# Second batch of a gated attention and expert kernel: another order of its query tiles, one more pair by seven products, and two tiles scored in one step

## The chip, the core and the metric

The kernel runs on one core of one Trainium2 chip. The core has a matrix engine (TensorE, PE in the profile), a vector engine (VectorE, DVE), a scalar engine (ScalarE, ACT), a general engine (GpSimd, POOL) and a synchronisation engine (SyncE, SP), which here issues nearly all the loads, stores and transposes by DMA. Each engine executes its own list of instructions in order and waits on semaphores for the others. The metric is device time in microseconds; the median of three runs before the change is 1007.83 us (1007.52 to 1008.42).

## What is computed

The input x has two batches of 2,048 tokens with 512 features. It is normalised twice over; causal attention with one head of width 512 and an output projection is taken of it, a mixture of eight experts (two per token) gives a gate, and the output is x plus attention times the gate:

```python
scores = jnp.einsum('bsk,btk->bst', q, k) * scale
scores = jnp.where(causal[None], scores, -jnp.inf)
attn = jax.nn.softmax(scores, axis=-1)
out = attn @ v
...
xn = _layernorm(x, axis=-1)
s = _L0_attn_ref(xn, ...)
g = _silu(_L0_ffn_ref(xn, ...))
x = x + s * g
```

Everything is computed in 32-bit floats. The change concerns the attention of the second batch only: `scores`, `attn` and `attn @ v`.

## The kernel before

**Stages.** The tokens are cut into 32 tiles of 128, sixteen to a batch, and into eight blocks of 512, four to a batch. Projections come first (queries, keys and values go to DRAM), then the routing, then the experts, and from about 550 us on the attention. The list of every engine is written out by hand: the order of the Python statements is the order of the instructions on each engine.

**The steps of the attention.** A loop (L1760) goes over steps `s` = 0 to 37. The list `seq` (L1014, L1015) says which query tile a step handles: steps 0 to 15 take the first batch from tile 15 down to tile 0, steps 16 to 31 the second batch in an order of its own. Steps go in pairs of neighbouring tiles, and pair numbers (`s // 2`) run from 0 to 15. Tile t of a batch needs t + 1 tiles of keys, so it has t + 1 units of score work and t + 1 units of value work.

**One plain step.** `chunk_scores` (L1302) multiplies the step's queries with a block of 512 keys, or what of it lies below the diagonal, into a PSUM bank of pool `ps_a` (five banks). VectorE masks the last 128 columns (L1312) and takes the maximum (L1295); `end_scores` (L1393) joins the maxima. `exponentials` (L1478) has ScalarE write the probabilities (L1485), POOL split them into 16-bit halves (L1495) and SP transpose them by DMA (L1501). In the step after, VectorE joins the transposed halves (`join_p`, L1515). Two steps after its scores, `values` (L1522) multiplies the transposed probabilities with the values into a bank of `ps_b` (three banks). The three smallest tiles are transposed by TensorE instead (`turn_p`, L1508).

**The end of a tile.** Three steps after its scores a tile is scaled (`attended`, L1693: ScalarE, then VectorE); in the step after that POOL multiplies and adds (`emit`, L1704) and SP stores. Every second step POOL gathers the experts' rows of a pair (`gather_y`, L1671), and later ScalarE and VectorE make the gate of them (`gate`, L1683), with a silu, for which ScalarE changes its table of functions.

**Seven products.** Pairs listed in `SCORED` (L1271) have the scores of their first 1,024 keys made by `fast_scores` (L1342). It takes the 2 x 2 blocks of a product (two query tiles by two key blocks, the 512 features in two halves) and makes seven half-size products in place of eight, from sums of the queries (`query_sums`, L1320, VectorE) and of two key blocks (`block_sums`, L1331). Pairs in `FAST` (L1272), which are those of `SCORED` and pair 4, have their values made by seven products too: `combine_v` (L1548) makes sums of a value block, `combine_p` (L1559) sums of the probabilities, and `values_first`, `values_next` and `values_end` (L1604 to L1622) the products and additions.

**Loads and sums in advance.** `parts_b` (L1740) lists the steps in which the second batch's key and value blocks are loaded, four parts a step; `later` (L1746) lists the steps in which their sums are made. Each entry names the steps of the four sums, the function and the block; K is the first block of the second batch.

Of the kernel before, what the change touches and what calls it, by code (L numbers as in the profile page):

```python
# [26 lines left out]
def gated_attention_moe(  # L27
# [32 lines left out]
    NT = B * S // P  # L60
    BT = 4
    TB = BT * P
    NB = NT // BT
    NBB = S // TB
# [947 lines left out]

    assert B == 2 and NBB == 4
    seq = [t for t in reversed(range(NBB * BT))]  # L1014
    seq += [NBB * BT + t for t in (8, 9, 0, 1, 6, 7, 2, 3, 4, 5, 10, 11, 12, 13, 14, 15)]  # L1015
    assert all(seq[s] // 2 == seq[s + 1] // 2 for s in range(0, NT, 2))
    fetch_k = fetch(aks, lambda: kp2, kt_d, "k2", "kT")
    fetch_v = fetch(avs, lambda: vp, v_d, "v2", "v")
# [249 lines left out]
    OUT = 4  # L1268


    SCORED = (0, 1, 2, 3, 13, 14, 15)  # L1271
    FAST = SCORED + (4,)  # L1272

    def place(s):
        b, t = divmod(seq[s], BT)
        return b, t, b - b % NBB
# [21 lines left out]
    def direct(s):  # L1298

        return range(2 if s // 2 in SCORED else 0, len(widths[s]))  # L1300

# [91 lines left out]
    def end_scores(s):  # L1393
        mx, nm, pieces = scored[s]
        nc.vector.tensor_reduce(nm, mx[:, : len(pieces)], AX.X, ALU.max, negate=True)  # L1395
# [82 lines left out]
    def exponentials(s):  # L1478

        _, nm, pieces = scored.pop(s)  # L1480
        rs = sm.tile([P, NBB], F32, name=f"rs_{s}", tag="rs")
        sums[s], halves[s] = rs[:, : len(pieces)], []
        for j, (src, at) in enumerate(pieces):
            end = at + src.shape[1]
            nc.scalar.activation(  # L1485
                turned[s][:, at:end], src, AF.Exp, bias=nm, accum_out=rs[:, j : j + 1]
            )
            if by_te(s):
                continue
            for k in range(at, end, TB):  # L1490
                w = min(end - k, TB)

                pool, tag, n = (op, "xo", 4) if s == 1 else (php, "pu", 3)
                pu = pool.tile([P, 2 * TB], U16, name=f"pu_{s}_{k}", tag=tag, bufs=n)
                nc.gpsimd.tensor_copy(  # L1495
                    pu[:, : 2 * w].rearrange("p (h d) -> p h d", h=2),
                    turned[s][:, k : k + w].bitcast(U16).rearrange("p (d h) -> p h d", h=2),
                )
                pool, tag, n = (op, "o", 4) if s == 1 else (php, "puT", 5)
                puT = pool.tile([P, 2 * BT, P], U16, name=f"puT_{s}_{k}", tag=tag, bufs=n)  # L1500
                nc.sync.dma_start_transpose(out=puT[:, : 2 * w // P, :], in_=pu[:, : 2 * w])  # L1501
                halves[s].append((puT, k, w))

    def by_te(s):

        return sum(widths[s]) <= 3 * P
# [186 lines left out]
    def attended(s):  # L1693
        n = seq[s]
        o = outs[s] if s // 2 in FAST else op.tile([P, D], F32, name=f"o_{s}", tag="o", bufs=4)
        nc.scalar.activation(  # L1696
# [42 lines left out]
    K = NBB  # L1739
# [6 lines left out]
    later = {}  # L1746
    for steps, f, b in (
        ((10, 10, 11, 11), combine_v, K + 2), ((12, 12, 13, 13), combine_v, K + 1),
        ((20, 21, 22, 23), block_sums, K), ((24, 25, 26, 27), combine_v, K),
    ):  # L1750
        for i, step in enumerate(steps):
            later.setdefault(step, []).append((f, b, (i + 1,)))
# [6 lines left out]

    for s in range(NT + OUT + 2):  # L1760
        fast = s // 2 - 1 in FAST
        pair = (s, s + 1) if s // 2 in SCORED else (s,)
        if s < NT and (s % 2 == 0 or len(pair) == 1):
            for k in pair:
                if s:
                    begin_scores(k)
                room(k)
        n = s // 2 + 1
        if s % 2 == 0 and NQ <= n < NT // 2:
            for c in range(2):  # L1770
                fetch_q(n, c)
        if s == 0:
            fetch_parts(s, NBB * ND)
            block_sums(0)
        late = []
        for k in range(NT):
            if k not in AHEAD:
                wait = 4 - k % 2 if k // 2 in FAST else 3
                if s == k + wait:
                    late.append((attended, k))  # L1780
                if s == k + wait + 1:
                    emit(k)
        if s == NT:

            values_first(s - 2)
            for k in AHEAD:
                make_ahead(k)
        if len(pair) == 1 or s % 2:
            for f, *args in late:
                f(*args)  # L1790
        for k in range(NT):
            if s == (NT - 1 if k in AHEAD else k + 2 - k % 2 if k // 2 in FAST else k + 1):
                fetch_inputs(k)
        if s == NT - 1:
            gather_y(NT - 2)
        if s % 2 and s > 3 and s // 2 + 1 in SCORED:
            query_sums(s + 1, nc.vector)
        joins = []
        for k in () if s == 1 else (0, 1) if s == 2 else (s - 1,):
            if 0 <= k < NT - 1 and not by_te(k):  # L1800
                joins += [(join_p, k)] * len(halves[k])
        chunks = []
        if s < NT and s != 1:
            chunks = [(k, j) for k in ((1,) if s == 0 else (s,)) for j in direct(k)]
        if s == 0:

            for k, j in chunks:
                chunk_scores(k, j)
            chunks = []
        if s < NT and s % 2 == 0 and len(pair) == 2:  # L1810
            pools = [(ps_a, "a")] * 5 + [(ps_b, "b"), (ps_a, "a")]
            if s < 3:
                pools = [(ps_b, "b")] * 3 + [(ps_a, "a")]
            if s == 2:
                joins = [(combine_v, b, (1,)) for b in range(NBB - 1)] + joins
            now = 5 if s == 2 else 1
            fast_scores(s, pools, late + joins[:now])
            joins = joins[now:]
            if s == 0:
                query_sums(2, nc.gpsimd)  # L1820
        for k, j in chunks:
            chunk_scores(k, j)
            if s != 3 and joins:
                f, *args = joins.pop(0)
                f(*args)
        if s != 3:
            for f, *args in joins:
                f(*args)
        if 0 <= s - 1 < NT and by_te(s - 1):

            if not fast:
                values(s - 2)
            turn_p(s - 1)
        if s < NT and s != 1:
            end_scores(s)
        if fast and s % 2 == 0 and 2 < s < NT:
            combine_p(s - 2)
        if 0 <= s - 1 < NT:
            divisor(s - 1)
        if s < NT:  # L1840
            if s != 1:
                exponentials(s)
            if s % 2 == 0 and len(pair) == 2:
                maximum(s + 1, turned[s + 1][:, : 2 * TB], 0)
            if s == 0:
                end_scores(1)
                exponentials(1)
            fetch_parts(s, 4)
            for f, *args in later.pop(s, []):
                f(*args)  # L1850
        if s == 2:
            pass
        elif s == 3:
            combine_p(0, (1, 3, 2))
            for b in range(NBB - 1):
                combine_v(b, (2,))
            values_first(0)
            combine_p(0, (4,))
            for b in range(NBB - 1):
                combine_v(b, (4,))  # L1860
            values_next(0)
            for f, *args in joins:
                f(*args)
            values_end(0, [lambda: query_sums(s + 1, nc.vector)])
        elif s == NT:
            emit_ahead(s - 2, seven[s - 2][1], LO)
            values_next(s - 2)
        elif fast and s % 2 == 0:
            values_first(s - 2)

            if s != NT - 2:
                values_next(s - 2)
        elif fast and s == NT - 1:
            values_next(s - 3)
            values_end(
                s - 3,
                [lambda: join_p(s)] * len(halves[s])
                + [lambda: combine_p(s - 1, (1, 3)), lambda: gate(s - 1)]
                + [lambda: combine_p(s - 1, (2, 4))],
            )  # L1880
        elif fast:
            values_end(s - 3)
        elif 0 <= s - 2 < NT and not (s - 1 < NT and by_te(s - 1)):
            values(s - 2)

        for k in range(0, NT - 2, 2):
            if s == (k + 2 if k + 2 in AHEAD else k + 3):
                gate(k)
        for k in range(0, NT - 2, 2):
            if s == k + 1:  # L1890
                gather_y(k)
        if s == 1:

            for b in (2, 0, 1):
                combine_v(b, (3,), nc.gpsimd)
# [45 lines left out]
```

## Time and profile before

The page shows one profiled execution. Its span is from the first to the last instruction; its own time is the device time of the same execution.

| what | value |
|---|---|
| median of three runs | 1007.83 us |
| profiled execution, its own time | 1007.83 us |
| its span | 1006.0 us |
| span outside the attention's last part | 0 to 568 us: TensorE busy 566.38 us |
| 568 to 777.3 us (the first batch's attention) | TensorE 208.65, VectorE 152.46, ScalarE 66.69, POOL 109.62 us of 209.3 |
| 777.3 to 865.6 us (the second batch's first ten steps) | TensorE 88.30, VectorE 53.45, ScalarE 43.02, POOL 66.69 us of 88.3 |
| 865.6 to 1002.2 us (its last six tiles) | TensorE 136.60, VectorE 103.32, ScalarE 45.28, POOL 66.48 us of 136.6 |

In the rows of the profile, L1307 stands for score work of a plain step, L1359 for the seven products of scores, L1535 for plain value work and L1583 for the seven products of values. A group such as "x8" of one score block has two rows for each matmul of 32-bit floats. An idle time in brackets names the engine and line that ended it.

### The profile page before, as it was taken

How to read it: one execution, taken by the hardware profiler on the slowest of the kernel's cores; microseconds unless marked ns; L12 is line 12 of the kernel's file. 1: busy time of each engine (PE TensorE's matmuls, PEld its weight loads, DVE VectorE, ACT ScalarE, POOL GpSimd, SP SyncE). 2: the span in 40 equal slices, each digit the busy share in tenths (PEclk: the TensorE clock that was granted, in tenths of full speed). 3: DMA queues.
4: the chain of work that ended last, by engine and by line, in shares of the span. 5: the costliest groups of instructions: out<-in, count | busy, mean ns of one | idle time of the engine just before them, and what ended most of it. 6: DMA issues, size and time to landing. Idle time of an engine off the chain costs nothing. (4 is left out here: it accounts for less than half of the span.)

```text
span 1006.0 us, 13431 instructions
## 1 busy us (share of the span) xinstructions
PE 999.9 (99%) x3924; PEld 665.3 (66%) x3924; DVE 716.9 (71%) x1396; ACT 403.2 (40%) x804; POOL 483.3 (48%) x475
## 2 busy tenths in 40 slices
PE   9999999999999999999999999999999999999998
PEld 5888888874567767766753448677675544447577
DVE  6996746897887777677744579668576556878667
ACT  3344445322444454444445112232335535442241
POOL 4474564004644454444332165254557776764272
PEclk9999999999999999999999999999999999999999
DMA  8689996978999999999999576274677768753361
GB/s 293 193 264 293 329 286 258 349 249 240 202 227 220 211 208 221 217 200 222 216 218 242 164 193 147 78 206 104 183 199 239 225 200 240 207 141 86 92 165 42
DMA packets 296647, 207.96 MB, mean 207 GB/s; under 512 B 230776, under 2 KB 243832, under 8 KB 296576
## 3 DMA queue, kind: packets, MB, share of 16 engines
q1 hardware_dynamic: 282432, 163.56, 63.2%
q0 software_dynamic: 10400, 34.63, 12.5%
q10 hardware_dynamic: 3744, 8.91, 2.4%
q8 instruction: 34, 0.56, 0.2%
q14 instruction: 37, 0.30, 0.1%
HBM read 92.35 MB, written 60.03 MB: 151 GB/s over the span
## 5 line engine op out<-in xcount | busy, mean ns | idle before, releaser
L1195 PE MATMUL py<-arena,ht 128*128 (+3 forms) x396 | 176.7, 593 | 0.0
L1307 PE MATMUL ps<-k,q 128*128 128x512 f32 (+3 forms) x416 | 143.0, 495 | 0.3 <-PEq L1455 0.3
L1495 POOL COPY pu<-pT 128x1024 uint16<-128x1024 uint16 (+2 forms) x74 | 82.5, 1146 | 118.1 <-ACT pT L1485 59.1
L1166 POOL COPY hu<-h 128x704 uint16<-128x704 uint16 x66 | 61.9, 956 | 155.8 <-issue 121.7
L1195 PEld LDWEIGHTS py<-arena,ht 128*128 128x128 f32 (+3 forms) x396 | 71.8, 185 | 80.7 <-issue 76.9
L1307 PEld LDWEIGHTS ps<-k,q 128*128 128x128 f32 x416 | 74.7, 190 | 67.1 <-issue 56.5
L970 POOL DMA_INDIRECT xs<-zu_d,toki x66 | 77.6, 1176 | 70.2 <-DVE toki L791 55.6
L1181 ACT ACTIVATE ht<-ht,b1sel 128x128 f32<-128x128 f32 (+3 forms) x216 | 67.9, 380 | 88.1 <-DVE ht L1175 88.1
L1145 DVE TENSOR_TENSOR h<-p,h 128x176 f32<-128x176 f32 x182 | 55.5, 337 | 60.7 <-PE p L1138 57.2
L1678 POOL DMA_INDIRECT yg<-y_d,posi x64 | 67.4, 1053 | 36.9 <-DVE yg L1689 21.9
L1535 PE MATMUL po<-v,pT 128*128 128x512 f32 x152 | 67.9, 592 | 0.0
L347 POOL COPY zu<-z 128x1024 uint16<-128x1024 uint16 x32 | 39.9, 1245 | 55.7 <-DVE z L332 55.7
L1517 DVE COPY pT<-puT 128x1024 uint16<-128x1024 uint16 (+2 forms) x74 | 54.1, 759 | 8.8 <-DMA puT<-pu 8.6
L1485 ACT ACTIVATE pT<-pT,nm 128x1024 f32<-128x1024 f32 x14 | 16.1, 1148 | 110.3 <-DVE nm L1395 72.0
L1203 ACT COPY y<-py 128x512 f32<-128x512 f32 x55 | 32.2, 585 | 62.3 <-PE py L1195 48.4
L1485 ACT ACTIVATE pT<-ps,nm 128x512 f32<-128x512 f32 (+3 forms) x52 | 30.1, 581 | 62.5 <-DVE nm L1395 38.8
L1365 DVE TENSOR_TENSOR pT<-p,pT 128x512 f32<-128x512 f32 x49 | 32.9, 687 | 25.8 <-PE p L1359 22.1
L1535 PEld LDWEIGHTS po<-v,pT 128*128 128x128 f32 x152 | 28.6, 190 | 31.9 <-issue 30.1
L1707 POOL TENSOR_TENSOR o<-o,yg 128x512 f32<-128x512 f32 x30 | 42.0, 1398 | 14.3 <-DVE o L1699 14.1
L1699 DVE SCALAR_TENSOR_TENSOR o<-xo,xscale,o 128x512 f32<-128x512 f32 x30 | 25.9, 871 | 30.1 <-ACT o L1696 30.1
L1046 DVE COPY xT<-xhT 128x1024 uint16<-128x1024 uint16 x66 | 45.2, 712 | 2.3 <-DMA xhT<-xs 2.0
L1708 POOL TENSOR_TENSOR o<-o,xo 128x512 f32<-128x512 f32 x30 | 43.0, 1432 | 2.4
(342 smaller groups left out, 2142.9 us busy)
## 6 DMA issues: line engine op xcount, KB each, us to landing
y_d<-y SPq DMA_DIRECT2D x66, 256.0 KB, 4.4
zu_d<-zu SPq DMA_DIRECT2D x32, 264.0 KB, 2.8
kt_d<-kT SPq DMA_DIRECT2D x16, 512.0 KB, 5.9
q<-qt_d SPq DMA_DIRECT2D x32, 256.0 KB, 5.4
k<-kt_d SPq DMA_DIRECT2D x32, 256.0 KB, 4.7
v<-v_d SPq DMA_DIRECT2D x32, 256.0 KB, 5.6
xo<-in_x_dram SPq DMA_DIRECT2D x32, 256.0 KB, 3.8
x<-in_x_dram SPq DMA_DIRECT2D x30, 256.0 KB, 4.9
```

The source lines that it names most:

```text
L970: nc.gpsimd.indirect_dma_start(out=xs, out_offset=None, in_=zu_d, in_offset=bass.IndirectOffsetOnAxis(ap=toki[:, order[i] : order[i] + 1], ...
L1046: nc.vector.tensor_copy(xT.bitcast(U16).rearrange("p c (t h) -> p c t h", h=2), xhs.pop(i).rearrange("p (h c) t -> p c t h", h=2),)
L1145: nc.vector.tensor_tensor(out, x, y, ALU.add)
L1166: nc.gpsimd.tensor_copy(hu[:, :, :H], h.bitcast(U16).rearrange("p (d h) -> p h d", h=2))
L1181: nc.scalar.activation(ht[:hn, c, at], ht[:hn, c, at], AF.Silu, bias=b1sel[:hn, c, j : j + 1])
L1195: nc.tensor.matmul(py[at, :], lhsT=ht[:k, c, at], rhs=rhs[n], start=(c == 0), stop=(c == NH - 1),)
L1307: nc.tensor.matmul(ps[:, :w], lhsT=aqs[seq[s] // 2][:, c, ts(t % 2, P)], rhs=aks[first + j][:, c, :w], start=(c == 0), stop=(c == ND - 1),)
L1485: nc.scalar.activation(turned[s][:, at:end], src, AF.Exp, bias=nm, accum_out=rs[:, j : j + 1])
L1495: nc.gpsimd.tensor_copy(pu[:, : 2 * w].rearrange("p (h d) -> p h d", h=2), turned[s][:, k : k + w].bitcast(U16).rearrange("p (d h) -> p h ...
L1517: nc.vector.tensor_copy(turned[s][:, k : k + w].bitcast(U16).rearrange("p (i t h) -> p i t h", t=P, h=2), puT[:, : 2 * w // P, :].rearrang ...
L1535: nc.tensor.matmul(dst, lhsT=turned[s][:, ts(k, P)], rhs=avs[first + k // BT][:, k % BT, cols], start=(start and k == k0), stop=(k == k1 - 1),
L1678: nc.gpsimd.indirect_dma_start(out=y, out_offset=None, in_=y_d, in_offset=bass.IndirectOffsetOnAxis(ap=posi[k][:, n : n + 1], axis=0),)
```

## The change

Four things are altered, all in the attention of the second batch.

- The order of its tiles is 4, 5, 0, 1, 2, 3, 8, 9, 6, 7, then 10 to 15 as before. It was 8, 9, 0, 1, 6, 7, 2, 3, 4, 5.
- Pair 11, which is now tiles 8 and 9, enters `SCORED`, and so `FAST`: scores of the first 1,024 keys and values are made by seven products.
- Pair 12, now tiles 6 and 7, is a new kind, `JOINT`: in its first step the scores, maxima and exponentials of both tiles are made, in its second step none.
- The key sums of block K are made in steps 14, 15 and 16 (they were in 20 to 23), its value sums in steps 17, 21 and 22 (they were in 24 to 27).

```diff
-    seq += [NBB * BT + t for t in (8, 9, 0, 1, 6, 7, 2, 3, 4, 5, 10, 11, 12, 13, 14, 15)]
+    seq += [NBB * BT + t for t in (4, 5, 0, 1, 2, 3, 8, 9, 6, 7, 10, 11, 12, 13, 14, 15)]
...
-    SCORED = (0, 1, 2, 3, 13, 14, 15)
+    SCORED = (0, 1, 2, 3, 11, 13, 14, 15)
     FAST = SCORED + (4,)
+    JOINT = (12,)
...
-        ((20, 21, 22, 23), block_sums, K), ((24, 25, 26, 27), combine_v, K),
+        ((14, 15, 16, 16), block_sums, K), ((17, 17, 21, 22), combine_v, K),
...
-        pair = (s, s + 1) if s // 2 in SCORED else (s,)
+        joint = s < NT and s // 2 in JOINT
+        pair = (s, s + 1) if s // 2 in SCORED or joint else (s,)
...
-        if len(pair) == 1 or s % 2:
+        if len(pair) == 1 or s % 2 or joint:
             for f, *args in late:
                 f(*args)
...
-            chunks = [(k, j) for k in ((1,) if s == 0 else (s,)) for j in direct(k)]
+            here = () if joint and s % 2 else pair if joint else (1,) if s == 0 else (s,)
+            chunks = [(k, j) for k in here for j in direct(k)]
...
-        if s < NT and s != 1:
-            end_scores(s)
+        for k in () if s >= NT or s == 1 or joint and s % 2 else pair if joint else (s,):
+            end_scores(k)
...
-            if s != 1:
-                exponentials(s)
-            if s % 2 == 0 and len(pair) == 2:
+            for k in () if s == 1 or joint and s % 2 else pair if joint else (s,):
+                exponentials(k)
+            if s % 2 == 0 and s // 2 in SCORED:
                 maximum(s + 1, turned[s + 1][:, : 2 * TB], 0)
```

More of the change, by code (lines that the diff above doesn't have):

```diff
@@ L1809, in gated_attention_moe @@
             chunks = []
-        if s < NT and s % 2 == 0 and len(pair) == 2:
+        if s < NT and s % 2 == 0 and s // 2 in SCORED:
             pools = [(ps_a, "a")] * 5 + [(ps_b, "b"), (ps_a, "a")]
```

## The prediction

> **What bounds the kernel now.** I read the page's busy shares first, then the chain of waits in order of time, then TensorE's own waits, then the timelines of the other engines between 752 and 930 us.
>
> ```profile
> PE 999.9 (99%) x3924; PEld 665.3 (66%) x3924; DVE 716.9 (71%) x1396; ACT 403.2 (40%) x804; POOL 483.3 (48%) x475
> ...
> PEclk9999999999999999999999999999999999999999
> ```
>
> TensorE is busy for 999.9 of 1006.0 us at full clock. "Busy" alone could hide slow matmuls, so look at who TensorE waited for in the whole program:
>
> ```profile
> PE warm L870 <- DVE b1s L181: 1.1, 1, 1.1
> PE p L1583 <- DVE u L1600: 0.4, 1, 0.4
> PE ps L1307 <- PEq L1455: 0.3, 1, 0.3
> PE pz L370 <- ACT zT L371: 0.3, 1, 0.3
> ```
>
> From 777.3 to 865.6 us, the ten steps that the change rearranges, TensorE was busy 88.30 of 88.30 us. So a column of matmul removed there is time won, and every gap opened there is time lost. The chain prices the columns (start, us, what; one matmul counts twice in these rows):
>
> ```profile
> 777.28 7.76 PE ps L1307 x24
> ...
> 797.21 7.73 PE po L1535 x18
> ...
> 806.66 8.58 PE po L1535 x20
> ...
> 893.22 12.02 PE p L1359 x28
> ...
> 909.56 4.32 PE p L1583 x20
> ```
>
> Below, S(s) is step s's score work and V(s) its value product. A 512-column matmul is 8.58/10 = 0.86 us, a 256-column one 4.32/10 = 0.43; S and V of tile t each take 0.86 x (t+1).
>
> **What it removes.** Tiles 8-9 go to seven products. Scores of their first 1,024 keys: four blocks of 3.43 us (the rows of eight) = 13.7 become 12.02, less 1.7. Values: 7.73 + 8.58 = 16.3 become 28 half-width matmuls (12.1) and six for the keys left over (2.6) = 14.7, less 1.6. **Together 3.3 us.** Reordering changes no other matmul. Without a new gap: 1007.83 - 3.3 = 1004.5.
>
> **What it adds beside TensorE.** VectorE gets four query sums, nine additions of the scores, four sums of probabilities, eight half-width additions; ScalarE two copies. All lie in steps 21 to 25; their price is when TensorE waits for them, below. The eight key and value sums for blocks 4-5 are moved, not added. At step 14 the first key sum (1.2 to 2.0 us in the rows of L1340) falls into VectorE's idle 1.92 us before 776.7; block 4 was issued at 764.1 and lands within 6 us, so it isn't waited for. The second meets 0.88 us of idle before the gating and delays that by about 0.3. The third and fourth fit before the first transpose lands at 790.7. Uncovered, each costs its 1.2 to 2.0. On SP the moved steps' input loads, query loads and stores keep their places relative to the transposes; block 4's values, issued at 778.1, land by 787, before V(16). The load of pair 8-9's queries stands behind step 15's store, which waits for POOL: issued at 806 to 808, landing 5.7 later (its row), it has about a microsecond to its first product at 814.5. The loads of the last block move with steps 20 and 22 and are wanted only at step 28. On POOL six steps with small tiles need about 36 us (two steps: 5.3 for outputs, 5.0 for gathers; pieces 5) against 33.5 of TensorE; it falls behind, but tiles 0 to 2 ask no piece of it.
>
> **What the order puts on the path.** Tile 8's scores used to be followed by tile 9's 8.6 us; now tile 4 comes first. Between S(16)'s end and V(16) TensorE has V(14) 1.72, a transpose 0.11, S(17) 5.16, V(15) 0.86, S(18) 0.89 = 8.7 us, where before it had 12. The path beside it is in these rows of the timelines:
>
> ```profile
> 789.32 2.82 POOL L1495 COPY pu<-pT 128x1024 uint16<-128x1024 uint16 x3 [1.35 <-ACT pT L1485]
> ...
> 793.69 1.57 DVE L1517 COPY pT<-puT 128x1024 uint16<-128x1024 uint16 x1 [1.21 <-DMA puT<-pu]
> ...
> 797.24 0.15 DVE L1395 TENSOR_REDUCE nm<-mx 128x1 f32<-128x3 f32 x1
> ...
> 800.57 1.28 ACT L1691 ACT_TABLE_LOAD   x1
> ...
> 803.63 0.75 DVE L1699 SCALAR_TENSOR_TENSOR o<-xo,xscale,o 128x512 f32<-128x512 f32 x1 [1.79 <-ACT o L1696]
> ...
> 804.84 3.31 DVE L1517 COPY pT<-puT 128x1024 uint16<-128x1024 uint16 x3
> ```
>
> From POOL's copy to the join behind the transpose: 793.69 - 789.32 = 4.37 us. From a tile's maximum to the next join on VectorE: 804.84 - 797.24 = 7.6, since exponentials, gating, table load, silu and one output stand in line between.
>
> *Wait A, V(16).* TensorE is ready at 777.28 + 4.32 + 8.74 = 790.3. VectorE finishes step 13's output at 783.2 in the trace, 783.5 with the delayed gating (issue to issue 0.67, so 784.2); maxima and mask 1.2, so the maximum at 785.6; exponential 0.8, so 786.4; copy and transpose 4.37, so 790.7; join 0.68, so **791.4: 1.0 us late** (0.5 to 1.9: the join took 0.68 alone, 1.57 beside POOL's work).
>
> *Wait B, V(17).* V(16) and S(19) take TensorE to 797.4. On VectorE mask, maximum and a short join of tile 5 are in line behind the first join: maximum at 792.5. The row's 7.6 less one exponential of three (0.9) gives 799.2, with the join 799.9: **2.5**. Two value sums now stand in this stretch beside ScalarE's exponentials; uncontended (0.68 each) they are hidden, at 1.09 to 1.43 each they push by up to 1.1. I take **2.7** (1.5 to 4.5).
>
> Then TensorE runs through to pair 8-9's first product at 814.5.
>
> *Wait C, the sums of pair 8-9.* Tile 3's scores hold a PSUM bank until their exponential, and on VectorE four query sums (mean 1.0 each in these rows, 0.41 alone) stand ahead of their maximum: the bank is free at 820.6, the fourth product wants it at 819.7. Gate 18's silu, behind that exponential, holds up the copy of the first product, so VectorE's additions begin about 824.9. In pair 10-11 they took 881.66 - 873.42 = 8.2 to the maximum: 833.1. Exponential 1.3, copy and three transposes 7.4 put the next maximum at 841.9; 6.4 us later (803.63 - 797.24) comes step 21's output, until 849.0; then the joint step's maxima, masks and three joins, 5.0 us by these rows, ahead of the two sums, 1.4: 855.4. TensorE has 12.9 us of joint scores and 3.9 of first value products as cover, and wants the sums at 851.9. **Late by 3.5**; if the additions began 7.8 us after the first product, as in pair 10-11 (873.42 - 865.59), everything is 2.6 earlier: 0.9. Ends 0 and 5; I take 3.0, nearer the long path because every link of it stands in the written order.
>
> Sum: 1007.83 - 3.3 + 1.0 + 2.7 + 3.0 = **1011.2**. The profiled execution's own time is 1007.83, span 1006.0 and 1.8 around it, and that is also the median of the runs, so nothing is to be corrected.
>
> [...]
>
> **Rivals.**
> *Only the columns count, 1004.5, faster (0.15).* For it: between 568 and 1006 us only 0.4 us of wait for VectorE, and tiles 5 to 0 already ran in sequence in the first batch without a gap. Against it: there, larger tiles went first, and 11.4 us from tile 3's scores (756.1) to its join (767.5) met 13.7 of cover, where tile 4 now has 8.7. It decides if the transposes' path is under 9 us.
> *A and B come, C is covered, 1008.2, no change (0.25).* One mechanism: VectorE catches up in the 12 us of seven products, as at pairs 10-11 and 12-13. It decides if the joint step's last maximum comes before 850.
> *The forecast, 1011.2 (0.45)*, its own range 1009.9 to 1013.5.
> *Contention lengthens all three, 1014.5 (0.15).* VectorE's join of 3.31 us for three shows what POOL beside it does[...].
> *That the seven products aren't made* can be left out: pair 11 enters the tuple that selects both paths.
>
> About 0.2% (2.0 us) is what a measurement of this kernel tells from no change, so faster means below 1005.8, slower above 1009.9. The cases give 0.15, 0.25 and 0.60. The range 1005.2 to 1015.0 takes in the covered case and most of the contended one.
>
> **What would show it.** L1359 gains 28 rows and the value rows of L1535 into po fall from 152 to 114, or the columns weren't saved. TensorE's waits should name VectorE's join (L1517) at about 790 and 797, and its sums (L1577) at about 852; the span between the fast pair's last product and its values would hold the rest. If TensorE's waits stay under 1.5 us in all, my layout of VectorE's queue is wrong. [...]

## The result and the profile after

The changed kernel takes **1020.20 us** (median of four runs, 1019.43 to 1020.71) against 1007.79 of the kernel before on the same chip: ratio 1.0122, 95% interval 1.0104 to 1.0139. Slower, as forecast, but by 12.4 us where 3.4 were forecast; the range ended at 1015.0. The profiled execution took 1020.39 us, its span is 1018.7.

First the page of the changed kernel, its busy shares and its clock row:

```profile
PE 1002.4 (98%) x3950; PEld 672.2 (66%) x3950; DVE 733.2 (72%) x1417; ACT 403.2 (40%) x802; POOL 484.5 (48%) x475
...
PEclk9999999999999999999999999999999899999999
```

TensorE is now idle for 16.3 us of the span instead of 6.1, and one slice of the clock row is no longer full. TensorE's own waits say for whom (line waited for: us in all, times, longest; every line number is one higher than before):

```profile
PE p L1584 <- DVE s L1578: 3.7, 1, 3.7
PE po L1536 <- issue: 3.4, 1, 3.4
PE ps L1308 <- DMA q<-qt_d: 2.3, 2, 1.2
...
PE po L1536 <- DVE pT L1518: 0.8, 1, 0.8
```

The same four waits in TensorE's timeline (start, us, what; in brackets the idle time ahead of it and what ended it):

```profile
788.92 1.02 PE L1536 MATMUL po<-v,pT 128*128 128x512 f32 x2
791.10 0.71 PE L1308 MATMUL ps<-k,q 128*128 128x128 f32 x4 [1.16 <-DMA q<-qt_d]
792.96 0.71 PE L1308 MATMUL ps<-k,q 128*128 128x128 f32 x4 [1.15 <-DMA q<-qt_d]
797.08 6.54 PE L1536 MATMUL po<-v,pT 128*128 128x512 f32 x10 [3.41 <-issue]
803.46 1.89 PE L1308 MATMUL ps<-k,q 128*128 128x256 f32 x8
806.12 5.39 PE L1536 MATMUL po<-v,pT 128*128 128x512 f32 x12 [0.77 <-DVE pT L1518]
...
862.22 3.41 PE L1584 MATMUL p<-vT,s 128*128 128x256 f32 x8 [3.67 <-DVE s L1578]
```

The order of the rows: score step S(18), tile 0, waits twice for its queries; V(16) waits for what the trace calls "issue" (the join behind the transposes ends in that instant, below); V(17) waits for its join; and the second value product of pair 8-9 waits for the sums of its probabilities. Together with 0.27 us inside the seven products of scores these are 10.4 us.

Look at the durations too: V(16), ten rows of tile 4, takes 6.54 us here and took 4.46 in the first batch. The windows of the changed kernel show why (window, its length, busy time and count of PE, PEld, DVE, ACT and POOL, granted clock, DMA share, GB/s):

```profile
783.00:791.00 8.00, 6.94 (x21) 3.48 (x19) 6.11 (x10) 4.96 (x9) 6.99 (x6) 1.00 0.98 338
...
790.90:794.31 3.41, 1.42 (x8) 1.04 (x8) 3.30 (x3) 0.00 (x0) 3.41 (x4) 1.00 0.70 224
794.31:797.73 3.42, 0.65 (x1) 0.50 (x2) 1.41 (x4) 0.00 (x0) 2.04 (x2) 0.50 0.62 143
797.73:801.14 3.41, 3.41 (x5) 1.35 (x4) 3.34 (x7) 3.18 (x7) 2.20 (x3) 0.50 0.31 109
801.14:804.55 3.41, 3.41 (x12) 1.91 (x11) 1.62 (x4) 3.02 (x4) 2.80 (x3) 1.00 0.88 196
```

The granted clock is 0.50 from 794.3, 0.6 us into the longest gap, to 801.1, and V(16) itself takes 2.1 us more than in the first batch; it is 0.50 again from 862.6 to 866.0, which costs the first two value products of pair 8-9 about 1.8 (5.21 us until the third begins at 867.43, for 16 rows that take 3.45 at full clock). In the kernel before the granted clock was 1.00 until 0.9 us before the end of the span (1005.1 of 1006.0).

**The account.** The seven products of pair 10-11 begin at 874.77 instead of 865.59, those of pair 12-13 at 905.68 instead of 893.06, those of the last pair at 944.88 instead of 932.26: the loss, 12.6 us, is complete by 906, and of the stretches from 777 to 875 nothing but the gaps, the clock and the columns is new (the values of tiles 6-7 now stand behind 875, those of 4-5 before it). Gaps 10.4, clock 3.9, a start 0.5 later at 777 (it is there at 690 already, ahead of anything changed), columns -3.3: 11.5. The rest lies at the edges of the gaps: a row's printed length reaches about 0.17 us into the next row (1.88 us are printed for four rows of which the next begins 1.72 later), so counted from start to start the gaps are 11.5 us, and the sum is 12.6.

**Where the first gap comes from.** POOL in the changed kernel:

```profile
780.27 2.13 POOL L1709 TENSOR_TENSOR o<-o,xo 128x512 f32<-128x512 f32 x1
...
786.62 0.95 POOL L1679 DMA_INDIRECT yg<-y_d,posi  x1 [0.30 <-issue]
787.59 1.28 POOL L1708 TENSOR_TENSOR o<-o,yg 128x512 f32<-128x512 f32 x1
788.95 2.13 POOL L1709 TENSOR_TENSOR o<-o,xo 128x512 f32<-128x512 f32 x1
791.03 2.83 POOL L1496 COPY pu<-pT 128x1024 uint16<-128x1024 uint16 x2
```

and in the kernel before:

```profile
778.91 1.27 POOL L1708 TENSOR_TENSOR o<-o,xo 128x512 f32<-128x512 f32 x1
...
784.40 0.94 POOL L1678 DMA_INDIRECT yg<-y_d,posi  x1 [0.30 <-issue]
785.35 1.27 POOL L1707 TENSOR_TENSOR o<-o,yg 128x512 f32<-128x512 f32 x1
786.71 1.26 POOL L1708 TENSOR_TENSOR o<-o,xo 128x512 f32<-128x512 f32 x1
```

POOL gathers the experts' rows of a pair and finishes an older tile before it splits tile 4's probabilities. It did that in the kernel before too, until 788.0; there tile 8's probabilities weren't wanted until 797. Now each second addition takes 2.13 instead of 1.27 us, and the piece begins at 791.03. VectorE's rows of the changed kernel show what ran beside it:

```profile
787.66 2.30 DVE L1341 TENSOR_TENSOR tk<-k 128x1024 f32<-128x1024 f32 x1
789.88 2.28 DVE L1341 TENSOR_TENSOR tk<-k,tk 128x1024 f32<-128x1024 f32 x1
792.08 1.52 DVE L1700 SCALAR_TENSOR_TENSOR o<-xo,xscale,o 128x512 f32<-128x512 f32 x1
...
796.29 0.69 DVE L1518 COPY pT<-puT 128x1024 uint16<-128x1024 uint16 x1 [2.08 <-DMA puT<-pu]
```

These are the third and fourth of the key sums that the change moved here. Last, SP's list:

```profile
782.43 0.34 SPq L1710 DMA_DIRECT2D out_dram<-o  x1
...
783.34 0.99 SPq L1007 DMA_DIRECT2D q<-qt_d  x2
...
793.09 2.53 SPq L1502 DMA_TRANSPOSE puT<-pu  x2
```

The load of S(18)'s queries stands behind a store that waits for POOL, and TensorE waits for its two halves until about 791 and 793, 8 and 9 us after issue, in a stretch where the DMA engines are busy for 98% of the time. In the kernel before they were as full (share 1.00, 365 GB/s between 783 and 791), and the same load, issued at 781.91, took as long (two loads, KB each, median us from issue to landing):

```profile
q<-qt_d SPq DMA_DIRECT2D x2, 256.0 KB, 8.5
```

But there S(18) began at 796.16: two steps of tiles 4 and 5 are 6.9 us shorter than two of tiles 8 and 9 (9.5 instead of 16.4), so TensorE comes to everything behind them 6.9 us earlier, while POOL, SP and the DMA engines have the same list of work.

The transposes were not slower. Of POOL's first copy and the transposes behind it, in the changed kernel and in the kernel before:

```profile
791.03 2.03 POOL L1496 COPY pu<-pT 128x1024 uint16<-128x1024 uint16 x1
...
789.32 1.03 POOL L1495 COPY pu<-pT 128x1024 uint16<-128x1024 uint16 x1 [1.35 <-ACT pT L1485]
...
790.38 3.90 SPq L1501 DMA_TRANSPOSE puT<-pu  x3
```

From the first transpose's issue to the join it is 3.2 us in the changed kernel (793.09 to 796.29) and 3.3 in the kernel before (790.38 to 793.69). POOL's first copy took 2.03 instead of 1.03, beside VectorE's last key sum.

### The profile page after: what moved, and what is told of

It is laid out like the page before. It is cut to its first block, busy times and chain, and to the rows that moved or that the text cites. A ratio compares the mean times of both kernels' runs of the same rounds, so it can differ in the third digit from the quotient of the medians.

```text
span 1018.7 us, 13501 instructions
## 1 busy us (share of the span) xinstructions
PE 1002.4 (98%) x3950; PEld 672.2 (66%) x3950; DVE 733.2 (72%) x1417; ACT 403.2 (40%) x802; POOL 484.5 (48%) x475
## 5 line engine op out<-in xcount | busy, mean ns | idle before, releaser
L1496 POOL COPY pu<-pT 128x1024 uint16<-128x1024 uint16 (+3 forms) x74 | 82.1, 1140 | 130.6 <-ACT pT L1486 69.3
L1308 PE MATMUL ps<-k,q 128*128 128x512 f32 (+3 forms) x384 | 129.4, 487 | 2.6 <-DMA q<-qt_d 2.3
L1308 PEld LDWEIGHTS ps<-k,q 128*128 128x128 f32 x384 | 68.6, 190 | 62.5 <-issue 47.6
L1486 ACT ACTIVATE pT<-pT,nm 128x1024 f32<-128x1024 f32 x16 | 18.4, 1148 | 127.9 <-DVE nm L1396 100.6
L1518 DVE COPY pT<-puT 128x1024 uint16<-128x1024 uint16 (+3 forms) x74 | 55.4, 779 | 9.2 <-DMA puT<-pu 9.0
L1366 DVE TENSOR_TENSOR pT<-p,pT 128x512 f32<-128x512 f32 x56 | 37.7, 688 | 31.6 <-PE p L1360 27.8
L1536 PE MATMUL po<-v,pT 128*128 128x512 f32 x114 | 53.4, 613 | 4.2 <-issue 3.4
L1486 ACT ACTIVATE pT<-ps,nm 128x512 f32<-128x512 f32 (+3 forms) x48 | 27.3, 571 | 51.5 <-DVE nm L1396 27.9
L1584 PE MATMUL p<-vT,s 128*128 128x256 f32 x180 | 43.3, 389 | 3.7 <-DVE s L1578 3.7
L1360 PE MATMUL p<-tk,sq 128*128 128x512 f32 x96 | 42.6, 593 | 0.1
```

The lines of the kernel that those rows point to most:

```text
L1308: nc.tensor.matmul(ps[:, :w], lhsT=aqs[seq[s] // 2][:, c, ts(t % 2, P)], rhs=aks[first + j][:, c, :w], start=(c == 0), stop=(c == ND - 1),)
L1360: nc.tensor.matmul(ps, lhsT=x[:, c], rhs=y[:, c], start=(c == 0), stop=(c == ND // 2 - 1))
L1496: nc.gpsimd.tensor_copy(pu[:, : 2 * w].rearrange("p (h d) -> p h d", h=2), turned[s][:, k : k + w].bitcast(U16).rearrange("p (d h) -> p h ...
L1518: nc.vector.tensor_copy(turned[s][:, k : k + w].bitcast(U16).rearrange("p (i t h) -> p i t h", t=P, h=2), puT[:, : 2 * w // P, :].rearrang ...
L1536: nc.tensor.matmul(dst, lhsT=turned[s][:, ts(k, P)], rhs=avs[first + k // BT][:, k % BT, cols], start=(start and k == k0), stop=(k == k1 - 1),
L1584: nc.tensor.matmul(dst, lhsT=a[:, k], rhs=v(k), start=(k == 0), stop=(stop and k == n - 1))
```

## The experiments

Eighteen variants were run, each beside the kernel before (1008.3 to 1008.5 us in these runs); where nothing is said it is a small edit of the kernel before.

**Which part costs what.** Order alone, and key sums alone (the value sums move with them):

```diff
-    ... (8, 9, 0, 1, 6, 7, 2, 3, 4, 5, 10, 11, 12, 13, 14, 15)]
+    ... (4, 5, 0, 1, 2, 3, 8, 9, 6, 7, 10, 11, 12, 13, 14, 15)]
```

> The kernel before with the new order of tiles alone: no pair more by seven products, no joint step, the sums in their old steps. Theory 1: with no key sums beside POOL in steps 14 to 16 the waits before V(16) are about 2.7 us and before V(17) 1 to 2, no clock loss; time 1011 to 1012.5. Rival (the order alone): waits of about 6.5 us and a clock loss of about 2 as in the changed kernel; time about 1016.

Measured 1015.92 (ratio 1.0078, 1.0060 to 1.0096), 7.5 us more with the same matmuls. This is the rival's time, though its waits are smaller: S(18) waits 1.7 for its queries, V(16) 2.3, and then V(16) is slow (7.21 us for its ten rows instead of 4.46; mean granted clock of the span 0.996, as against 1.000 in the kernel before).

```diff
-        ((20, 21, 22, 23), block_sums, K), ((24, 25, 26, 27), combine_v, K),
+        ((14, 15, 16, 16), block_sums, K), ((17, 17, 21, 22), combine_v, K),
```

> The kernel before with the early key and value sums alone, old order, no pair more by seven products. Theory 1: POOL's outputs of steps 14 and 15 stretch to about 2.1 us here too and tile 8's first piece starts about 791, but tile 9's 8.6 us of scores cover it: time 1007.8 to 1009. If the sums cost TensorE time by themselves, over 1010.

Measured 1010.54 (1.0022, 1.0010 to 1.0034), so 2.1 us more, within 1.0 and 3.4. POOL's rows in this kernel, with the old order:

```profile
780.58 2.13 POOL L1708 TENSOR_TENSOR o<-o,xo 128x512 f32<-128x512 f32 x1
...
789.24 2.14 POOL L1708 TENSOR_TENSOR o<-o,xo 128x512 f32<-128x512 f32 x1
791.33 3.82 POOL L1495 COPY pu<-pT 128x1024 uint16<-128x1024 uint16 x3
```

The additions take 2.13 again and the piece starts 2.0 us later than before (0.8 of it this execution had lost by 690, ahead of anything changed) and its three copies take 3.82 us instead of 2.82. Nothing was changed but the moment of the sums: with VectorE's sums in these steps (at 780.27, 788.55 and 790.18) POOL's additions at 780.58 and 789.24 take 2.13 and 2.14 us, where those at 778.91 and 786.71 in the kernel before take 1.27 and 1.26. TensorE waits 0.3 us at V(16) and 1.3 at V(17), for joins behind that piece. If the parts add, 7.5 for the order, 2.1 for the sums and 2.6 for the new pair (a wait of 3.8 from start to start and 1.8 of half clock at its sums, 0.3 among its products, less 3.3 of columns) are 12.2 of the 12.4 us.

The other direction, the whole change with the key sums at steps 18 to 21:

> The changed kernel with the four key sums of block K in steps 18 to 21 in place of 14 to 16; all else as changed. Theory 1 (the early key sums hold up POOL: its output operations take 2.1 us beside them and 1.3 without, and POOL's line then holds up a store, the query load of pair 9 behind it on SP, and tile 4's piece): POOL should start tile 4's piece about 788 and not 791, the waits before V(16) fall from 5.7 us to about 2.7, [...]the clock row keeps full speed near 800; time about 1016. Rival (the new order alone leaves too little cover, the sums' place is nothing): waits before V(16) stay above 5 us, time within 1 us of 1020.2. Of the sums near step 21, up to 2 us more in front of pair 8-9's maximum by both.

Measured 1022.05 (1.0144, 1.0118 to 1.0170), not the 1016 expected. POOL's piece was back at 788.01 and V(16)'s and the queries' waits fell to 3.0, but the query sums of pair 8-9 now came 2.0 us late behind the key sums, and the mean granted clock of the span was 0.993, as against 0.995 in the changed kernel. And the whole change without its joint step (`JOINT = ()`):

> The changed kernel with pair 12 scored one tile a step. If the joint step is what makes VectorE late for pair 8-9's sums of probabilities, the wait of 3.7 us and the slow clock after it go: about 1015. If the lateness comes from before it (tile 8's and 9's transposes and the gating in front of step 21's output), the sums come only about 2.5 us sooner while TensorE arrives 6.9 us sooner: the wait grows to about 8 us, time about 1024.

Measured 1026.18 (1.0173, 1.0156 to 1.0190): the wait for the sums of pair 8-9 grows from 3.7 to 9.5. The joint step is cover, not cause. Part of the wait of 3.7 comes from the output of an older tile, which the change puts ahead of the joint step's maxima; put behind the sums:

```diff
-        if len(pair) == 1 or s % 2 or joint:
+        if len(pair) == 1 or s % 2:
             for f, *args in late:
                 f(*args)
...
+        if joint and s % 2 == 0:
+            for f, *args in late:
+                f(*args)
         if 0 <= s - 1 < NT:
             divisor(s - 1)
```

> The changed kernel with step 21's output scaled behind the sums of probabilities of pair 8-9 in the joint step, not ahead of the step's maxima. Theory (VectorE stands idle 1.8 us in front of that output, which waits for the silu on ScalarE, and everything behind it waits too): the sums come about 2.5 us sooner, the wait before them falls from 3.7 to about 1.2 us and the clock keeps full speed there: about 1016. Rival (the joins of tile 9 come late anyway): wait and time stay within 1 us.

Measured 1018.08 (1.0087, 1.0053 to 1.0121). The wait fell to 2.1 and the clock stayed full at 860 (mean of the span 0.997 instead of 0.995): 2 us won, not 4.

**Which line holds V(16) and V(17)?** With the order alone, POOL's outputs of steps 16 and 17 behind the step's pieces:

```diff
-                if s == k + wait + 1:
+                if s == k + wait + 1 and s not in (16, 17):
                     emit(k)
...
+            if s in (16, 17):
+                emit(s - 4)
             fetch_parts(s, 4)
```

> The kernel before with the new order of tiles alone, and in steps 16 and 17 POOL's two output operations (and their stores) put behind the step's pieces in place of ahead of them. Theory (POOL's line, gathers and an output, is what holds tile 4's piece until 787.8): the piece starts about 786.2 as soon as its exponential is there, V(16) is ready about 791.2, so the wait of 2.3 us before it goes and only the query wait of 1.7 stays; without the second gap the clock stays at full speed: 1010 to 1011. Rival (ScalarE or the transposes set it): V(16)'s wait stays over 1.5 us and the time within 1 us of 1015.9.

Measured 1016.12 (1.0074, 1.0047 to 1.0101): nothing won. The piece moved from 787.84 to 785.77 and the transposes went out at 786.83, but the join came only at 793.14, 6.3 us later, where 3.2 us are enough for the later ones of the changed kernel: 1 MB of values, the queries and the gathers had been issued in the 9 us ahead of the transposes. With the values of block K also loaded behind the queries, at step 16:

> As order_pieces_first, and block K's values (1 MB) are loaded behind the query load of pair 9 and not ahead of it. Theory (that load's 9 us come from the megabyte ahead of it on the same DMA engines): the queries land by 788, S(18) doesn't wait, V(16) then waits about 1 us for its join; 1009 to 1010. Rival (the query load is late because it is issued late, behind a store that waits for POOL): its wait stays about 1.7 us, time as order_pieces_first. If the values now come late, V(16) waits for DMA.

Measured 1016.94 (1.0076, 1.0049 to 1.0103). The queries were no longer waited for; V(16) waited 4.3 us instead, since now the values lay ahead of the transposes. So the values were loaded earlier, at the start of step 14, without and with POOL's edit:

```diff
-... (14, fetch_v, K)
+... (13.5, fetch_v, K)
...
+        if s == 14:
+            fetch_parts(s, 4)
         late = []
```

> The kernel before with the new order of tiles alone, and block K's values (1 MB) put ahead of step 10's store on SP, so that they start about 770 and not 779. Theory (DMA engines full from 779 to 791 are the second thing that holds step 16 to 18: the megabyte lies ahead of pair 9's queries and tile 4's transposes): queries land in under 6.5 us, S(18) doesn't wait, the first transpose lands in under 3.7 us and not 5, V(16) starts about 792.8: 1012.5 to 1014. Rival (POOL's line alone): V(16) starts where it did, 794.8, time 1015.9 within 1 us.

> Both together: the values early, and POOL's output operations of steps 16 and 17 behind the pieces. Theory (POOL's line and DMA's line hold tile 4 one behind the other, so that undoing one bares the other): the piece starts at 785.8, its transpose lands about 790.2, V(16) waits about 1.3 us, no slow clock: 1009.5 to 1011. Rival (something else holds V(16)): over 1013.

Measured 1015.13 (1.0064, 1.0048 to 1.0081) and 1015.90 (1.0074, 1.0058 to 1.0091). In the second the transposes landed 3.5 us after issue instead of 6.3, the queries weren't waited for, and V(16) was 1.7 us late and took 4.53 us for its ten rows. The time hardly moved: V(17) came 2.3 us earlier than with the order alone (803.61), waited 3.0 us and then took 8.29 us for twelve rows, which take 5.31 with the order alone (mean granted clock of the span 0.997):

```profile
792.03 4.53 PE L1535 MATMUL po<-v,pT 128*128 128x512 f32 x10 [1.72 <-DVE pT L1517]
796.39 1.89 PE L1307 MATMUL ps<-k,q 128*128 128x256 f32 x8
801.32 8.29 PE L1535 MATMUL po<-v,pT 128*128 128x512 f32 x12 [3.03 <-DVE pT L1517]
```

VectorE's lines of the same kernel show the third path, the one of the forecast's wait B:

```profile
799.28 0.75 DVE L1699 SCALAR_TENSOR_TENSOR o<-xo,xscale,o 128x512 f32<-128x512 f32 x1 [1.79 <-ACT o L1696]
...
800.48 1.03 DVE L1517 COPY pT<-puT 128x1024 uint16<-128x1024 uint16 x2
```

The join stands behind an output that waits for ScalarE's table load (1.28), silu (1.06) and scaling (0.76). In the whole change with every line mended so far (values early, pieces first, key sums at 17 to 20, output behind) it was the same:

> The changed kernel with the values early, the pieces ahead of the outputs in steps 16 and 17, key sums in steps 17 to 20, and step 21's output behind the sums of probabilities. If these lines are the cause, the waits before V(16) fall from 5.7 to about 1.3 us, the wait before the sums of pair 8-9 to 1 to 2, of the clock's loss nothing is left, and the 3.3 us of columns are won: 1009 to 1012. If over 1014, a wait that I don't know has come up.

Measured 1018.22 (1.0101, 1.0085 to 1.0118), with waits of 2.0, 2.2, 1.4 and 2.0 us and slow value products after the first two (V(16) took 6.23 us for ten rows; mean granted clock of the span 0.997). So the outputs of steps 17 to 20 were put behind the joins:

```diff
-        if len(pair) == 1 or s % 2:
+        if (len(pair) == 1 or s % 2) and not 17 <= s <= 20:
             for f, *args in late:
                 f(*args)
...
+        if 17 <= s <= 20 and (len(pair) == 1 or s % 2):
+            for f, *args in late:
+                f(*args)
         if 0 <= s - 1 < NT and by_te(s - 1):
```

> The new order alone with block 4's values issued at step 14 and POOL's outputs of steps 16 and 17 behind the pieces, as before, and with one more edit: in steps 17 to 20 the output of an earlier tile (the VectorE instructions that wait for ScalarE's silu) stands behind the joins of the step. If the round trip from VectorE's gating to ScalarE's silu and back is what pins the start of V(17) at 801 to 803, the wait before it falls from 3.03 to about 1 us, the clock stays full after it, and the time falls from 1015.9 to about 1011 (2.0 less of wait, 1.7 to 3 less of slow matmul). If something else pins it (the transposes of tile 5, the exponential of tile 5), the wait stays at 2.5 to 3 and the time at 1015 to 1016.

> The whole change with every line of the path mended (values early, pieces first, sums later, step 21's output behind the sums) and the earlier outputs behind the joins in steps 17 to 20. Round trip theory: V(17) waits under 1.2 us instead of 2.17, the clock drop at 803 goes, 1018.2 becomes about 1013. If another line pins it: 1018.

Measured 1018.59 (1.0111, 1.0084 to 1.0137) and 1017.41 (1.0098, 1.0078 to 1.0118). TensorE's waits in the first of them:

```profile
PE ps L1307 <- ACT pT L1485: 2.7, 1, 2.7
PE po L1535 <- DVE pT L1517: 2.2, 1, 2.2
PE ps L1307 <- DVE ri L1659: 1.4, 1, 1.4
```

From tile 5's maximum to its join VectorE now takes 6.2 us instead of 7.8, and the join comes with the landing of the transposes (799.47): in the order alone the round trip was the last line there, by 1.6 us. That V(17) waits for nothing is due to the slow V(16) too, which took 6.25 us for its ten rows, 1.7 longer than the 4.53 above. The 2.2 is V(16), the 1.4 stands at 816 behind outputs that are now late in their turn, and the 2.7 at 836, where VectorE stands 8.6 us idle for transposes that land 9.7 us after their issue. The sum of waits is 6.2 us instead of 4.8. In the whole change the wait before V(17) rose to 2.6, now behind ScalarE.

**Other orders.** If the tiles' order is the cause, an order with more cover should be free. Pairs 6-7, 0-1, 4-5, 2-3, 8-9, with the last by seven products, no joint step and the key sums at their old place; then 6-7, 0-1, 2-3, 4-5, 8-9 with values early and pieces first as well; then that with the outputs behind the joins:

> Another placing of the same seven products: second batch in the order 6, 7, 0, 1, 4, 5, 2, 3, 8, 9, 10 to 15, pair 8-9 by seven products just ahead of pair 10-11, which has 12 us of seven products itself; no joint step; key sums in steps 20 to 23 as before, value sums in 24 and 25. If cover is all that was missing, 3.3 us of columns are won and little is lost: S(16) to V(16) has 10.4 us of cover and no wait of TensorE should be over 1.5 us: 1005 to 1007. If tile 6's piece is still held by POOL until 788 and joined at 792.4, V(16) waits under 1 us. Against it: over 1008 if the pairs in between wait for their transposes.

> Order 6, 7, 0, 1, 2, 3, 4, 5, 8, 9, 10 to 15, pair 8-9 by seven products just ahead of pair 10-11, no joint step, sums in steps 20 to 25, the values early and the pieces ahead of the outputs in steps 16 and 17. Longer tiles open the batch and stand ahead of the seven products: waits of TensorE in the second batch 1 to 3 us in all against 3.3 us of columns won: 1005.5 to 1008.5. If VectorE is late at pair 8-9's query sums again, waits of 1 to 2 us there and 1009 to 1010.

> The order 6, 7, 0, 1, 2, 3, 4, 5, 8, 9 with pair 8-9 still by seven products, values early and pieces first, and the earlier outputs behind the joins in steps 17 to 20. Round trip theory: the waits before V(17) and V(21) (1.86 and 3.88) shrink to under 1.5, no slow matmul is left, about 1009 to 1012. If the outputs aren't the cause: 1017 again.

Measured 1015.94 (1.0070, 1.0052 to 1.0089), 1017.45 (1.0101, 1.0072 to 1.0130) and 1017.22 (1.0092, 1.0076 to 1.0109), none as expected. In the first no wait exceeds 2.1 us, but there are seven between 0.2 and 2.1 (V(16), V(17), V(20), V(21), two in the products of scores, the sums of pair 8-9), and the mean granted clock of the span is 0.998. In the other two it is V(21) that is 3.9 and 4.0 late and then slow (mean granted clock 0.997 in both).

Last the falling order, 8-9, 6-7, 4-5, 2-3, 0-1, alone and with the whole change (pair 8 in `SCORED`, `JOINT = (9,)`, key sums at steps 14 and 15, value sums at 16 and 17):

> The kernel before with another order alone: 8, 9, 6, 7, 4, 5, 2, 3, 0, 1, 10 to 15, so that every tile from 9 down is followed by work of tiles near its own size. Cover theory: between a tile's scores and its values TensorE has the next two score steps and two value products; for tile 4 that is then V(6) 6.0, S(5) 5.2, V(7) 6.9, S(2) 2.6 = 20.7 us instead of the 8.7 of the changed order, for tile 5 about 13, and tiles 3 to 0 need no DMA transpose. So no wait over 1 us and a full clock: 1007 to 1010. If it is any change of order that costs (loads and stores meeting differently): 1014 to 1016, as all other orders gave.

> The whole change with the falling order: 8-9 by seven products at steps 16 and 17, 6-7 with both tiles' scores in one step right behind, then 4, 5, 2, 3, 0, 1; key sums at steps 14 and 15, value sums at 16 and 17. Cover theory: the small tiles' waits are gone and the columns stay saved; the sums of the first probabilities are waited for by about 2 to 4 us with a drop of the clock, since step 17's output and three joins stand ahead of them: 1004.5 + 2.1 (key sums beside POOL) + 3 to 5 = 1009 to 1012. If the order isn't the cause: 1018 to 1020.

> As falling_seven, with the output of the joint step behind the sums and block 4's values issued at the start of step 14. Cover theory: the wait for the sums falls by about 1.5 us and the clock stays full there: 1006 to 1009. If the order isn't the cause: 1017 or more.

Measured 1016.53 (1.0082, 1.0065 to 1.0099), 1026.19 (1.0166, 1.0146 to 1.0186) and 1022.50 (1.0134, 1.0117 to 1.0151). With the order alone TensorE has no gap at all between 778 and 870, which is what cover promised for tiles 8 to 4. The gap comes where the small tiles now stand:

```profile
855.63 3.60 PE L1307 MATMUL ps<-k,q 128*128 128x512 f32 x8
859.06 5.31 PE L1535 MATMUL po<-v,pT 128*128 128x512 f32 x12
864.21 0.49 PE L1512 MATMUL pt<-ident,pT 128*128 128x128 f32 x3
864.54 1.06 PE L1307 MATMUL ps<-k,q 128*128 128x128 f32 x8
865.43 2.74 PE L1535 MATMUL po<-v,pT 128*128 128x512 f32 x6
868.01 1.89 PE L1307 MATMUL ps<-k,q 128*128 128x256 f32 x8
872.28 3.67 PE L1535 MATMUL po<-v,pT 128*128 128x512 f32 x8 [2.37 <-DVE ri L1659]
```

Tile 3's scores end at 859.1, its values begin at 872.3: a path of 13 us that met 10.8 of cover. Behind that gap the eight rows take 3.67 us, as at full clock (3.60 for the eight at 855.63), and the mean granted clock of the span is 1.000. (The expectation had tile 3 among those that TensorE transposes; only tiles 0 to 2 are.) Two more waits, 2.4 and 1.3 us, stand in the next pair's products of scores at 906 and 911. With the whole change the sums of queries and of keys, which now stand right ahead of their products, come 2.0 and 0.9 us late as well, and those of the probabilities 6.5 us (3.6 with the output behind them). The profiled execution of the former, 1032.55, had also lost some 5 us near 277, ahead of the attention.

**What follows.** Tile 3 gives a measure. From the end of its scores to its values the first batch left 13.7 us (its pairs run 3, 2 and not 2, 3) and the kernel before 19.3 in the second, both without a wait; the falling order left 10.8, and the changed order left tile 4 8.7. From a tile's scores to its values the path beside TensorE took 10.6 to 13.5 us for tile 4 in the order alone and its mendings, 13.2 for tile 3 in the falling order and 15.2 for tile 4 in the changed kernel, whichever of its lines was last. In the order before, 8-9, 0-1, 6-7, 2-3, 4-5, the larger tiles lie between the small ones so that every one of them whose transposes go by DMA gets 11.2 us or more, and none waits. In the order alone tile 4 gets 8.7; the gaps ahead of its values, their edges and the slow value product behind them are all of its 7.5 us, with not one matmul more. In the falling order tile 3's gap is 2.4 of 8.2 us and 3.7 stand in the next pair's products of scores, so the cover of one tile is not all of it there. For the two orders between them, with their many small waits, it was not followed tile by tile. No version beat the kernel before. That no other order can is not shown; the order before with seven products for pair 8-9 wasn't tried.

## Why the prediction was wrong

**Columns, right.** The value rows into po fell from 152 to 114 and L1360 has 28 rows more; the predicted 3.3 us are in the account.

**Wait A, the step that failed.** Forecast 1.0 us, from VectorE's list alone: output, maxima, exponential, then "copy and transpose 4.37". It took 5.7 (queries 2.3, V(16) 3.4), and V(16) then ran 2.1 longer. Two lines were left out of that term. POOL's: the row of its gathers and outputs until 788.0 was in the trace before, and by it alone the copy could not begin at 786.4; it began at 791.03, and took 1.0 us longer. The prediction reckoned POOL's load over six steps ("falls behind, but tiles 0 to 2 ask no piece of it") and not its queue at the moment when tile 4 asks. And the DMA queue's, in "keep their places relative to the transposes": the query load kept its place, but its first use moved 6.9 us forward. The trace before had its landing 8.5 us after issue, between 790 and 791, and by the prediction's own sum S(18) now wanted it at 789.4 (790.3 less its 0.89). For tile 4's transposes that queue was not the last line here, since POOL held them until 793.1; it became so when POOL had been mended and they went out at 786.8 (6.3 us).

**Key sums, wrong.** "Fit before the first transpose lands" asked only for VectorE's time, and that was too short as well: the first two sums made tile 4's maximum 1.9 us late (787.5 instead of 785.6, 0.5 of it the later start; 0.3 was forecast), which POOL's queue hid. Beside them POOL's additions went from 1.27 to 2.13 us, which with the old order, the value sums moved too, costs 2.1 us by itself, and here puts tile 4's piece from 788.0 to 791.0.

**Wait B, right.** From tile 5's maximum (797.76) to its join (805.28) VectorE took 7.5 us; the forecast took 6.9, the row's 7.6 less an exponential and 0.2 for the value sums, with up to 0.9 more in its range. TensorE waited only 0.8 instead of 2.7, since the slow V(16) filled 2.1 of it: 2.9 together. With the order alone the slow V(16) (7.21 us) filled all of it, and where V(16) took 4.53 us V(17) waited 3.0. That is why mending A's lines won nothing: with the order alone and its first four mendings V(17) began between 801.3 and 804.4, and in the earliest case ran slow.

**Wait C, right, without its clock.** 3.7 against 3.0, and along the path as worked out (VectorE's additions begin 10.4 us after the first product in both): the output ahead of the joint maxima is worth 1.6 of it. The half clock behind it, 1.8, is the next point.

**The clock, left out of the sum.** The first slow stretch of the changed kernel began at 794.3, when the long gap had lasted 0.6 us; in the 3.41 us ahead of it TensorE was busy for 1.42, and 1.35 of the rest were the waits for queries. The second began at 862.6; in the 3.41 us ahead of it TensorE was busy for 0.36. The two stretches, 6.8 and 3.4 us at 0.50, cost 2.1 and 1.8 us, for which the forecast's sum has no term. V(16) was slow as well behind gaps of 2.0 us in the mended whole change and 2.2 with the order's joins first (6.23 and 6.25 us for ten rows instead of 4.53), and not behind the 1.7 of the order with values early and pieces first. What decides when the clock falls wasn't shown. The table load is 1.28 us in these rows too, as the forecast took it.

**Rivals.** "Contention", 1014.5, was nearest in mechanism: POOL beside VectorE, and long waits with a slow clock behind them. It was priced on B and not on A, and at 0.15 much too low. POOL's row alone, read in the trace before, would have put A's copy at 788.0, V(16) at 788.0 + 4.37 + 0.69 = 793.1, 2.8 late, and the sum at 1013.0. Of the 9.2 us that were missed, 4.7 are A, 0.2 B with the slow V(16) inside it, 0.9 the sums of pair 8-9 with the 0.27 us among the products of its scores, 1.8 the half clock behind those sums, 0.5 the later start and 1.1 the edges of the gaps and the rest.

## What to carry to other kernels

Before a step is pulled forward, list for the new moment what every engine and every DMA queue still has in front of it; a tile that arrives 7 us earlier finds each of these lists as long as it was, and its time is set by the last of them. Undoing one of several parallel lines wins little (here POOL's, the DMA queue's and the round trip's were undone in turn), so look at the cover of an order's shortest stretch and not only at its sum of work; that this alone ranks orders is not shown. A gap of TensorE could cost more than its length here: behind waits of 5.7 and 3.7 us the changed kernel lost another 2.1 and 1.8 to a granted clock of 0.50, and behind waits of 1.7 and 2.3 the order alone 2.8 in V(16), but behind 2.37 us the falling order lost nothing to it. Price such a loss as possible and not certain.

## What the runs showed of the hardware

- The granted clock of the changed kernel was 0.50 from 794.3 to 801.1 and from 862.6 to 866.0, and 1.00 in the rest of the attention. Ten rows of value work took 6.54 us across the first stretch, and 4.46 in the first batch. The kernel before, with no wait over 0.4 us between 568 and 1002, had 1.00 up to 1005.1. Not every wait was followed by a slow stretch: behind 1.74 and 2.30 us with the order alone ten rows took 7.21 us, and behind 2.37 us in the falling order eight took 3.67, with a mean granted clock of the span of 0.996 and 1.000.
- POOL's addition of two 128x512 operands took 1.26 us while VectorE stood idle (at 786.71 in the kernel before) and 2.13 beside VectorE's key sums of 128x1024 (at 788.95 in the changed kernel). The key sums took 1.20 us at their shortest in the kernel before, and 2.30 and 2.28 here.
- With POOL's pieces first, transposes were joined 3.5 us after their issue when the values had been loaded early and 6.3 when 1 MB of values, the queries and the gathers had been issued in the 9 us ahead of them; in the changed kernel, where they went out 6 us later, 3.2. The two query loads of 256 KB took 8 to 9 us in the changed kernel, 8.5 in the same place before, and 5.7 in the row that the forecast used.
